# Stretches of a two-layer graph kernel ordered by a clock per engine, the first pair's addend rows made by TensorE, the other rows' transfers on the sync queue

## The chip, the cores and the metric

The kernel runs on one core of one Trainium2 chip. The metric is the device time of one execution in microseconds. All runs used here were in the fast state; most executions of one kernel agree within 0.3%. A profile's span is some 2 us shorter than the time of the run that it was taken from.

## The reference, cut to what matters

64 graphs of 256 nodes with 256 features go through two layers. Layer one is two graph attentions (GAT), a layer norm and a feed-forward with Relu; layer two is an attention with 8 heads, a layer norm and a feed-forward with Gelu.

```python
# layer 0, twice: graph attention
e = leaky_relu(Wh1 + swapaxes(Wh2, 1, 2), 0.2)
att = softmax(where(adj > 0, e, NEG), axis=1);  h = att @ Wh
# ... layer norm, Relu feed-forward of width 1024, layer norm
# layer 1: attention of 8 heads, masked by adj == r, for r in 0..3
# ... layer norm, Gelu feed-forward of width 1024, layer norm
```

## The kernel before

The kernel takes the graphs in 32 pairs. Each pair is a Python generator that emits its instructions in stretches; `in_turn` keeps three pairs under way and picks, at every `yield`, whose stretch comes next. This fixes the order of instructions on each engine when the program is built. A `yield us, later, needs` says how long TensorE is thought to take and how long after that the pair can go on.

```python
    def in_turn(ways, together):
        now, going = 0.0, []
        # ... fill `going` with up to `together` pairs
            ready = [g for g in able if g[1] <= now] or [min(able, key=lambda g: g[1])]
            g = min(ready, key=lambda g: g[2] == "ff" or alone.get("ff") is g[0])
            # ...
            us, later, needs = step
            now = max(now, g[1]) + us
            g[1:] = now + later, needs
```

A GAT's weights need one exponential per node along a row, the same on all 128 partitions. They are formed as a column, turned on VectorE, written to DRAM and read back replicated:

```python
    def addends(y, at, layer, pair):
        # ...
        for b in range(2):
            e1 = y[:, of_graph(b), at]
            nc.scalar.activation(of_kind[:, 2 * b], e1, AF.Exp, bias=shift[:, 0:1])
            nc.scalar.activation(of_kind[:, 2 * b + 1], e1, AF.Exp, bias=shift[:, 0:1], scale=ALPHA)
        nc.scalar.activation(ratio, y[:, :, at + 1], AF.Exp, scale=ALPHA - 1.0)
        blocks = small.tile([P, 2, 32], F32, name="blocks")
        nc.vector.transpose(blocks.rearrange("p j c -> p (j c)"), rise.rearrange("p j c -> p (j c)"))
        row = scratch.tile([2, 16, 32], F32, name="row")
        nc.gpsimd.dma_start(row.rearrange("j q c -> q j c"), blocks[0:P:8])
        rows = work.tile([P, 8, 4, 32], F32, name="rows")
        nc.gpsimd.dma_start(rows.rearrange("p q n c -> p (q n c)"), row.rearrange("j q c -> (j q c)").partition_broadcast(P))
        return rows, ratio
```

Feed-forwards and attention begin with rows transposed on TensorE and copied out of PSUM by ScalarE. That copy, `yT`, matters below, and so does the activation of the feed-forward, whose function is Relu in layer one and Gelu in layer two:

```python
    def rows_transposed(y, needs):
        yT = work.tile([P, KC, 512], F32, name="yT", bufs=3)
        for b in range(2):
            # ... four nc.tensor.transpose into pt
            nc.scalar.activation(yT[:, :, b * N:(b + 1) * N], pt.rearrange("p (c n) -> p c n", c=KC), AF.Copy)
            yield 0.5, 0.5 + b * 0.8, needs if b else None
        return yT

    def feed_forward(y, w, func, gb):
        # ...
            nc.scalar.activation(h, p1, func, bias=b1[:, m:m + 1])
```

## Time and profile before

| | before |
|---|---|
| time, median of the first 3 runs (lowest to highest) | 3348.53 us (3345.63 to 3352.18) |
| span of the profile | 3344.5 us |
| TensorE busy | 3283.8 us, 98% |
| longest waits of TensorE | 18.3 and 14.2 us, both in the first pair |
| one pair in the middle | some 101.9 us |

How to read it: TensorE is full but for 60.7 us, and the two waits are more than half of that. The prediction shows the lines that carry this. One group that it did not look at is ScalarE's loading of function tables. In this view of groups (line, engine, operation, count, then busy us and mean ns, then idle time before) the kernel before has:

```profile
L343 ACT ACT_TABLE_LOAD x75 | 96.2, 1283 | 6.6 <-PE ps L340 5.3
L397 ACT ACT_TABLE_LOAD x46 | 59.0, 1283 | 0.8
L223 ACT ACT_TABLE_LOAD x28 | 35.9, 1283 | 0.5
```

A switch from Exp to Gelu or back costs ScalarE 1.28 us each time, 150 times in all with the load at the start. No wait of TensorE in the middle follows from them here.

### The profile page before, as it was taken

The page shows a single profiled execution, that of the slowest core. Times are in us where ns is not written, and L with a number is a line of the kernel's source. Part 1 is how long each engine was busy: PE and PEld are TensorE (multiplying, and loading weights), DVE is VectorE, ACT ScalarE, POOL GpSimd, SP SyncE. Part 2 cuts the span into 40 slices and gives each one's busy share as a digit, 9 for nine tenths or more (in the row PEclk, how much of TensorE's full clock was granted, in tenths as well). Part 3 has the DMA queues.
Part 4 walks back from the last instruction along what each step waited for, and adds up shares of the span by engine and source line. Part 5 has one row for each costly group of instructions (what it writes and reads, how often), then busy time and mean ns, then how long its engine had stood idle before and what let it go on. Part 6 is the DMA issues. An engine that isn't in the chain of part 4 may idle for free.

```text
span 3344.5 us, 45688 instructions
## 1 busy us (share of the span) xinstructions
PE 3283.8 (98%) x18270; PEld 2106.0 (63%) x18270; DVE 1836.8 (55%) x4835; ACT 1263.6 (38%) x2326; POOL 275.7 (8%) x390
## 2 busy tenths in 40 slices
PE   4999999999999999999999999999999999999998
PEld 3666666666665656666666666566666666666665
DVE  3655465654555654556545656545555455665444
ACT  2334333343433343333343333443344433434422
POOL 0000010000000000100000100001000001000000
PEclk7999999999999999999999999999999999999999
DMA  6000111010111011110011110101110010100000
GB/s 190 32 7 32 39 38 32 20 32 32 39 35 36 13 36 35 39 32 25 28 32 38 39 32 14 38 32 38 32 32 20 32 39 32 39 7 26 20 7 14
DMA packets 78556, 111.95 MB, mean 33 GB/s; under 512 B 6784, under 2 KB 61184, under 8 KB 78336
## 3 DMA queue, kind: packets, MB, share of 16 engines
q1 hardware_dynamic: 67072, 75.13, 7.2%
q0 software_dynamic: 11264, 33.82, 2.9%
q8 instruction: 146, 2.39, 0.3%
q14 instruction: 74, 0.61, 0.1%
HBM read 91.90 MB, written 17.04 MB: 33 GB/s over the span
## 4 chain that ended last, share of the span: by engine, by line
PE 94%; DMA 3%; DVE 2%; ACT 1%; issue 0%; POOL 0%; SPq 0%; POOLq 0%; DVEq 0%
PE ps L351 26%; PE ps L340 25%; PE ps L420 6%; PE ps L367 6%; PE ps L374 6%; PE ps L392 4%; PE ps L413 4%; PE ps L289 4%; PE ps L261 3%; PE ps L437 3%; PE ps L274 3%; PE ps L327 2%; DMA rows<-row 1%; DMA adjT<-in_adjT 1%; DMA row<-blocks 1%; DVE e L240 0%
## 5 line engine op out<-in xcount | busy, mean ns | idle before, releaser
L340 PE MATMUL ps<-yT,w_L_gnn_W 128*128 128x512 f32 x1024 | 471.6, 597 | 0.7 <-ACT yT L329 0.7
L351 PE MATMUL ps<-w_L_gnn_W,ff 128*128 128x256 f32 x2048 | 457.9, 379 | 0.0
L351 PE MATMUL ps<-w_L_gnn_w_ff,ff 128*128 128x256 f32 x2048 | 455.2, 379 | 0.0
L340 PE MATMUL ps<-yT,w_L_gnn_w_ff 128*128 128x512 f32 x1024 | 452.7, 595 | 0.7 <-ACT yT L329 0.7
L351 PEld LDWEIGHTS ps<-w_L_gnn_w_ff,ff 128*128 128x128 f32 x2048 | 389.0, 190 | 66.6 <-issue 15.3
L351 PEld LDWEIGHTS ps<-w_L_gnn_W,ff 128*128 128x128 f32 x2048 | 384.3, 190 | 51.8 <-issue 2.1
L312 POOL TENSOR_TENSOR rstd<-rstd,mhalf 128x2 f32<-128x2 f32 x256 | 202.9, 793 | 2493.2 <-DVE rstd L311 2478.5
L397 ACT ACTIVATE a<-ps 128x512 f32<-128x512 f32 x512 | 264.3, 602 | 350.1 <-PE ps L392 349.9
L406 DVE TENSOR_TENSOR m<-a,adjT 128x512 f32<-128x512 f32 x512 | 325.2, 685 | 120.3 <-ACT a L397 107.3
L302 DVE TENSOR_TENSOR x<-ps,x 128x512 f32<-128x512 f32 x256 | 172.2, 673 | 330.7 <-PE ps L351 309.3
L340 PEld LDWEIGHTS ps<-yT,w_L_gnn_w_ff 128*128 128x128 f32 x1024 | 192.8, 191 | 218.1 <-issue 208.2
L329 ACT ACTIVATE yT<-ps 128x512 f32<-128x512 f32 x192 | 113.8, 594 | 566.1 <-PE ps L327 564.6
L340 PEld LDWEIGHTS ps<-yT,w_L_gnn_W 128*128 128x128 f32 x1024 | 183.7, 190 | 185.7 <-issue 176.7
L343 ACT ACTIVATE ff<-ps,c_L_gnn_b 128x512 f32<-128x512 f32 x256 | 175.6, 686 | 327.3 <-PE ps L340 326.8
L240 DVE SCALAR_TENSOR_TENSOR e<-rows,ratio 128x256 f32<-128x256 f32 x256 | 116.3, 477 | 322.7 <-DMA rows<-row 314.8
L343 ACT ACTIVATE ff<-ps,c_L_gnn_b_ff 128x512 f32<-128x512 f32 x256 | 175.9, 687 | 269.6 <-PE ps L340 269.5
L369 DVE TENSOR_TENSOR v<-ps,b_L_gnn_bv 128x512 f32<-128x512 f32 x128 | 87.5, 684 | 286.4 <-PE ps L367 286.4
L367 PE MATMUL ps<-wv,yT 128*128 128x512 f32 x512 | 235.4, 592 | 0.0
L426 DVE RECIPROCAL s<-ps 128x256 f32<-128x256 f32 x128 | 224.1, 1751 | 0.0
L309 DVE BATCH_NORM_STATS2 st<-x 128x6 f32<-128x256 f32 x512 | 192.3, 416 | 6.1
L247 ACT ACTIVATE xw<-xw,rs 128x258 f32<-128x258 f32 (+1 forms) x256 | 117.4, 502 | 144.0 <-DVE rs L244 144.0
L367 PEld LDWEIGHTS ps<-wv,yT 128*128 128x128 f32 x512 | 97.2, 190 | 114.3 <-issue 113.4
(97 smaller groups left out, 3763.9 us busy)
## 6 DMA issues: line engine op xcount, KB each, us to landing
rows<-row POOLq DMA_DIRECT2D x64, 512.0 KB, 3.9
xT<-in_xT SPq DMA_DIRECT2D x32, 512.0 KB, 4.2
adjT<-in_adjT SPq DMA_DIRECT2D x32, 512.0 KB, 3.9
x<-in_x SPq DMA_DIRECT2D x32, 512.0 KB, 3.9
out<-x SPq DMA_DIRECT2D x32, 512.0 KB, 2.9
w_L_gnn_w_ff<-in_L_gnn_w_ff SPq DMA_DIRECT2D x2, 1024.0 KB, 9.6
w_L_gnn_W<-in_L_gnn_W SPq DMA_DIRECT2D x2, 1024.0 KB, 11.6
row<-blocks POOLq DMA_DIRECT2D x64, 4.0 KB, 1.9
```

The lines of the kernel that those rows point to most:

```text
L302: nc.vector.tensor_tensor(rows, p, rows, ALU.add)
L309: nc.vector.bn_stats(st[:, j, :], r[:, 2 * b + j, :])
L312: nc.gpsimd.tensor_tensor(rstd, rstd, mhalf[:, :2], ALU.pow)
L340: nc.tensor.matmul(p1, lhsT=w1[:, c, m * P:(m + 1) * P], rhs=yT[:, c, :], start=c == 0, stop=c == KC - 1)
L343: nc.scalar.activation(h, p1, func, bias=b1[:, m:m + 1])
L351: nc.tensor.matmul(p2[:, j * D:(j + 1) * D], lhsT=f[m][:, k * P:(k + 1) * P], rhs=w2[:, m, :], start=m == 0, stop=m == NF - 1)
L367: nc.tensor.matmul(ps, lhsT=yT[:, c, at:at + P], rhs=wv[:, c].rearrange("p r m -> p (r m)"), start=c == 0, stop=c == KC - 1)
L374: nc.tensor.matmul(ps, lhsT=w[:, d, c * P:(c + 1) * P], rhs=yT[:, d, :], start=d == 0, stop=d == KC - 1)
L397: nc.scalar.activation(a, ps[o], AF.Exp)
L406: nc.vector.tensor_tensor(m, a, adj, ALU.mult)
L420: nc.tensor.matmul(po[o * DH:(o + 1) * DH, :N], lhsT=v[:, jc, at:at + DH], rhs=ms[o][:, jc * N:(jc + 1) * N], start=r == 0 and jc == 0, st ...
L426: nc.vector.reciprocal(s, po[:, N:])
```

## The change

It has three parts. Part 1: the rows of the first pair, which has no other work to stand beside its transfers, come from TensorE: a transpose of a broadcast column yields the same row on all partitions. Part 2: the order follows a clock per engine. A stretch reports when each engine would be done with its results, and the pair goes on then. Part 3: the other pairs' row transfers are issued on the sync queue in place of GpSimd's. The diff, cut to its core:

```diff
+    clock = {"tensor": 0.0, "vector": 0.0, "scalar": 0.0, "gpsimd": 0.0}
+    def took(us):
+        clock["tensor"] += us
+        return clock["tensor"]
+    def after(ready, *work):
+        for engine, us in work:
+            ready = clock[engine] = max(ready + 0.2, clock[engine]) + us
+        return ready
 # in in_turn
-            ready = [g for g in able if g[1] <= now] or [min(able, key=lambda g: g[1])]
+            ready = [g for g in able if g[1] <= clock["tensor"]] or [min(able, key=lambda g: g[1])]
 # in addends
+        if pair == 0:
+            for n in range(4):
+                p = bank()
+                for j in range(2):
+                    nc.tensor.transpose(p[:, j * P:(j + 1) * P], rise[:, j, 8 * n:8 * n + 1].to_broadcast([P, P]), ident)
+                nc.scalar.activation(rows[:, :, n], p[:, :N].rearrange("p (q c) -> p q c", q=8), AF.Copy)
+            return rows, ratio, after(took(1.6), ("scalar", 2.0))
-        nc.gpsimd.dma_start(row.rearrange("j q c -> q j c"), blocks[0:P:8])
-        nc.gpsimd.dma_start(rows.rearrange("p q n c -> p (q n c)"), row.rearrange("j q c -> (j q c)").partition_broadcast(P))
-        return rows, ratio
+        nc.sync.dma_start(row.rearrange("j q c -> q j c"), blocks[0:P:8])
+        nc.sync.dma_start(rows.rearrange("p q n c -> p (q n c)"), row.rearrange("j q c -> (j q c)").partition_broadcast(P))
+        return rows, ratio, after(clock["tensor"], ("scalar", 2.2), ("vector", 0.4)) + 6.6
 # in feed_forward; the other yields change alike
-            yield 1.72, 0.0, None
+            there = after(took(1.72), ("scalar", 0.7))
+            yield clock["tensor"] if m < NF - 1 else max(clock["tensor"], there - 3.0), None
 # ... cut: the same for gat_layers, layernorm, rows_transposed, attention, whole_way
```

The clock counts 0.7 us of ScalarE for a feed-forward tile. It knows no function tables.

More of the change, by code (lines that the diff above doesn't have):

```diff
@@ L174, in relieve_attention, with each_after @@
         nc.vector.tensor_tensor(bv, bv, p, ALU.subtract)
+    clock = {"tensor": 0.0, "vector": 0.0, "scalar": 0.0, "gpsimd": 0.0}
     alone = {}
+    def took(us):
[5 more added lines that the diff above has]
+        return ready
+    def each_after(ready, times, *work):
+        for _ in range(times):
+            end = after(ready, *work)
+        return end
     def in_turn(ways, together):
-        now, going = 0.0, []
-        ways = iter(ways)
+        going, ways = [], iter(ways)
         while True:
@@ L196, in in_turn @@
                 alone[g[2]] = g[0]
+            clock["tensor"] = max(clock["tensor"], g[1])
             step = next(g[0], None)
@@ L199, in in_turn @@
                 going.remove(g)
-                continue
-            us, later, needs = step
-            now = max(now, g[1]) + us
-            g[1:] = now + later, needs
+            else:
+                g[1:] = step
     def done_with(name):
@@ L225, in addends @@
         nc.scalar.activation(ratio, y[:, :, at + 1], AF.Exp, scale=ALPHA - 1.0)
+        rows = work.tile([P, 8, 4, 32], F32, name="rows")
+        if pair == 0:
[5 more added lines that the diff above has]
+            return rows, ratio, after(took(1.6), ("scalar", 2.0))
         blocks = small.tile([P, 2, 32], F32, name="blocks")
@@ L228, in addends @@
         row = scratch.tile([2, 16, 32], F32, name="row")
-        nc.gpsimd.dma_start(row.rearrange("j q c -> q j c"), blocks[0:P:8])
-        rows = work.tile([P, 8, 4, 32], F32, name="rows")
-        nc.gpsimd.dma_start(rows.rearrange("p q n c -> p (q n c)"), row.rearrange("j q c -> (j q c)").partition_broadcast(P))
-        return rows, ratio
+        nc.sync.dma_start(row.rearrange("j q c -> q j c"), blocks[0:P:8])
+        nc.sync.dma_start(rows.rearrange("p q n c -> p (q n c)"), row.rearrange("j q c -> (j q c)").partition_broadcast(P))
+        return rows, ratio, after(clock["tensor"], ("scalar", 2.2), ("vector", 0.4)) + 6.6
     def gat_weights(y, at, rows, ratio, adjT, empty, b):
@@ L247, in gat_weights @@
             nc.scalar.activation(y[:, k, :at], y[:, k, :at], AF.Copy, scale=rs[:, j:j + 1])
-        return e
+        return e, after(clock["tensor"], ("vector", 2.3), ("scalar", 1.0))
     def gat_layers(pair, xT, adjT, x):
@@ L263, in gat_layers @@
                 nc.scalar.activation(y[:, k], ps[:, :D + 4], AF.Copy)
+            took(1.75)
             if b == 0:
-                yield 1.75, 0.0, None
-        rows, ratio = addends(y, D + 2, 0, pair)
-        yield 1.75, 8.6, None
+                yield clock["tensor"], None
+        rows, ratio, there = addends(y, D + 2, 0, pair)
+        yield there, None
         e = [gat_weights(y, D + 2, rows, ratio, adjT, empty, b) for b in range(2)]
-        yield 0.0, 4.6, None
+        yield e[0][1], None
         for b in range(2):
@@ L273, in gat_layers @@
                 for j in range(2):
-                    nc.tensor.matmul(ps[:, :D + 2], lhsT=e[b][:, j, i * P:(i + 1) * P], rhs=y[:, 2 * b + j, :D + 2],
+                    nc.tensor.matmul(ps[:, :D + 2], lhsT=e[b][0][:, j, i * P:(i + 1) * P], rhs=y[:, 2 * b + j, :D + 2],
                                      start=j == 0, stop=j == 1)
                 nc.scalar.activation(z[:, 2 * b + i, :D + 2], ps[:, :D + 2], AF.Copy)
+            took(1.75)
             if b == 0:
-                yield 1.75, 0.4, None
-        rows, ratio = addends(z, D, 1, pair)
+                yield e[1][1], None
+        rows, ratio, there = addends(z, D, 1, pair)
         if pair + 1 < NPAIR:
             loaded[pair + 1] = load(pair + 1)
-        yield 1.75, 8.6, None
-        e += [gat_weights(z, D, rows, ratio, adjT, empty, b) for b in range(2)]
-        yield 0.0, 4.6, None
+        yield there, None
+        e = [gat_weights(z, D, rows, ratio, adjT, empty, b) for b in range(2)]
+        yield e[0][1], None
+        normal = []
         for b in range(2):
@@ L288, in gat_layers @@
                 for j in range(2):
-                    nc.tensor.matmul(ps[:, i * D:(i + 1) * D], lhsT=e[2 + b][:, j, i * P:(i + 1) * P],
+                    nc.tensor.matmul(ps[:, i * D:(i + 1) * D], lhsT=e[b][0][:, j, i * P:(i + 1) * P],
                                      rhs=z[:, 2 * b + j, :D], start=j == 0, stop=j == 1)
+            took(1.75)
             add_rows(x, ps, b)
-            layernorm(x, ln[0], b)
+            normal.append(layernorm(x, ln[0], b))
             if b == 0:
-                yield 1.75, 0.4, None
+                yield e[1][1], None
         done_with("gat")
-        yield 1.75, 6.0, None
+        return normal
     def add_rows(y, p, b):
@@ L318, in layernorm, with rows_transposed @@
             nc.vector.scalar_tensor_tensor(row, row, rstd[:, j:j + 1], beta, op0=ALU.mult, op1=ALU.add)
-    def rows_transposed(y, needs):
+        return after(clock["tensor"], ("vector", 2.0), ("gpsimd", 1.0), ("vector", 1.8))
+    def rows_transposed(y, normal, needs):
         yT = work.tile([P, KC, 512], F32, name="yT", bufs=3)
         for b in range(2):
+            yield normal[b], None
             pt = bank()
@@ L329, in rows_transposed, with feed_forward @@
             nc.scalar.activation(yT[:, :, b * N:(b + 1) * N], pt.rearrange("p (c n) -> p c n", c=KC), AF.Copy)
-            yield 0.5, 0.5 + b * 0.8, needs if b else None
+            there = after(took(0.45), ("scalar", 0.6))
+        yield there, needs
         return yT
-    def feed_forward(y, w, func, gb):
+    def feed_forward(y, normal, w, func, gb):
         w1, b1, w2 = w
-        yT = yield from rows_transposed(y, "ff")
+        yT = yield from rows_transposed(y, normal, "ff")
         f = []
@@ L352, in feed_forward @@
                                      start=m == 0, stop=m == NF - 1)
-                if k < 3:
-                    if j == 1:
-                        add_rows(y, p2, b)
-                        layernorm(y, gb, b)
-                    yield 3.44, 0.0, None
-        add_rows(y, p2, 1)
-        layernorm(y, gb, 1)
+                took(3.44)
+                if j == 0:
+                    yield clock["tensor"], None
+            add_rows(y, p2, b)
+            normal[b] = layernorm(y, gb, b)
+            if b == 0:
+                yield clock["tensor"], None
         done_with("ff")
@@ L369, in values @@
         nc.vector.tensor_tensor(v[:, jc], ps, bv, ALU.add)
+        return after(took(1.72), ("vector", 0.7))
     def projected(to, c, yT, w, bias, scale):
@@ L375, in projected, with attention @@
         nc.scalar.activation(to[:, c, :], ps, AF.Identity, bias=bias[:, c:c + 1], scale=scale)
-    def attention(y, pair, adjT):
-        yT = yield from rows_transposed(y, "attention")
+        return after(took(1.72), ("scalar", 0.7))
+    def attention(y, normal, pair, adjT):
+        yT = yield from rows_transposed(y, normal, "attention")
         qT, kT, oT = (work.tile([P, KC, 512], F32, name=n) for n in ("qT", "kT", "oT"))
@@ L398, in scores @@
                 e.append(a)
+            took(0.95)
             return e
@@ L407, in of_relation_1 @@
                 ms.append(m)
-            return ms
+            return ms, each_after(clock["tensor"], HQ, ("scalar", 0.62), ("vector", 0.62))
         def sums(e, po):
@@ L430, in divided @@
             nc.vector.tensor_tensor(oT[:, c, b * N:(b + 1) * N], po[:, :N], s, ALU.mult)
+            return after(clock["tensor"], ("vector", 2.6))
         def into_rows(b):
@@ L438, in into_rows @@
                                      start=c == 0, stop=c == KC - 1)
+            took(1.72)
             add_rows(y, ps, b)
-        groups = [(b, c) for b in range(2) for c in range(KC)]
+        divisions, groups = [], [(b, c) for b in range(2) for c in range(KC)]
         v = values_tile()
         projected(qT, 0, yT, wq, bqs, SCALE)
-        projected(kT, 0, yT, wk, bk, 1.0)
-        yield 3.44, 0.0, None
+        there = projected(kT, 0, yT, wk, bk, 1.0)
+        yield clock["tensor"], None
         values(v, 0, 0, yT)
-        yield 1.72, 0.0, None
+        yield there, None
         e = scores(*groups[0])
-        ms = of_relation_1(0, e)
+        ms, masked = of_relation_1(0, e)
         projected(qT, 1, yT, wq, bqs, SCALE)
-        yield 3.0, 0.0, None
-        projected(kT, 1, yT, wk, bk, 1.0)
-        values(v, 1, P, yT)
-        yield 3.44, 0.0, None
+        yield clock["tensor"], None
+        there = projected(kT, 1, yT, wk, bk, 1.0)
+        there = max(there, values(v, 1, P, yT), masked)
+        yield there, None
         for n, (b, c) in enumerate(groups):
@@ L463, in attention @@
             if not last:
-                e, ms = ahead, of_relation_1(groups[n + 1][0], ahead)
-            divided(b, c, po)
-            if last:
-                layernorm(y, ln[2], 0)
-            yield 3.1 if last else 4.1, 4.8 if last else 0.8, None
+                e, (ms, masked) = ahead, of_relation_1(groups[n + 1][0], ahead)
+            took(2.65)
+            divisions.append(divided(b, c, po))
             if n == 0:
@@ L471, in attention @@
                 for jc in range(2):
-                    values(following, jc, N + jc * P, yT)
-                    yield 1.72, 0.0, None
+                    yield clock["tensor"], None
+                    there = values(following, jc, N + jc * P, yT)
             if n == 1:
@@ L476, in attention @@
             if n == 2:
+                yield divisions[1], None
                 into_rows(0)
-                yield 1.75, 0.0, None
+            if last:
+                normal[0] = layernorm(y, ln[2], 0)
+            yield divisions[3] if last else max(masked, there), None
         into_rows(1)
-        layernorm(y, ln[2], 1)
+        normal[1] = layernorm(y, ln[2], 1)
         done_with("attention")
-        yield 1.75, 6.0, None
     def whole_way(pair):
-        yield 0.0, 0.0, "gat"
+        yield 0.0, "gat"
         xT, adjT, x = loaded.pop(pair)
-        yield from gat_layers(pair, xT, adjT, x)
+        normal = yield from gat_layers(pair, xT, adjT, x)
         if pair == 0:
             relieve(ff0[1], ff0[0], ln[0][2])
-        yield from feed_forward(x, ff0, AF.Relu, ln[1])
-        yield 3.44, 6.0, None
+        yield from feed_forward(x, normal, ff0, AF.Relu, ln[1])
         if pair == 0:
             relieve_attention(ln[1][2])
-        yield from attention(x, pair, adjT)
+        yield from attention(x, normal, pair, adjT)
         if pair == 0:
             relieve(ff1[1], ff1[0], ln[2][2])
-        yield from feed_forward(x, ff1, AF.Gelu, ln[3])
-        yield 3.44, 5.0, None
+        yield from feed_forward(x, normal, ff1, AF.Gelu, ln[3])
+        yield max(normal), None
         nc.sync.dma_start(out[2 * pair:2 * pair + 2].rearrange("b (c p) d -> p (b c) d", p=P), x)
```

## The prediction

> **What bounds the kernel now.** I read four views in order: the page's busy table and slices, who waited for whom on TensorE, TensorE's timeline in the first 100 us, and the chain of waits at the end.
>
> ```profile
> PE 3283.8 (98%) x18270; PEld 2106.0 (63%) x18270; DVE 1836.8 (55%) x4835; ACT 1263.6 (38%) x2326; POOL 275.7 (8%) x390
> ...
> PE   4999999999999999999999999999999999999998
> ...
> PEclk7999999999999999999999999999999999999999
> ```
>
> TensorE (PE) is busy for 3283.8 of 3344.5 us, so all that a better order can win without removing matmuls is the rest, 60.7 us, or 1.8% of the time. The second row says where most of it lies: 38 of 40 slices are full, the first (83.6 us) is 4 tenths busy. In two inner periods of 101.8 us that I measured (1710 to 1913.6 us), PE was busy for 203.43 of 203.60 us.
>
> ```profile
> PE ps L274 <- ACT xw L247: 18.3, 1, 18.3
> PE ps L289 <- ACT xw L247: 14.2, 1, 14.2
> PE pw L121 <- DVE junk L115: 7.5, 1, 7.5
> PE ps L327 <- DVE x L318: 1.9, 1, 1.9
> PE ps L340 <- ACT yT L329: 1.4, 2, 0.7
> ```
>
> Columns: waiter, releaser, total us, times, longest. Two single waits make 32.5 us. They name ScalarE's scaling (L247), but that is only the last link; the timeline of PE dates them:
>
> ```profile
> 12.17 5.41 PE L261 MATMUL ps<-w,xT 128*128 128x260 f32 x16 [0.84 <-DVE w L123]
> 35.83 5.50 PE L274 MATMUL ps<-xw,e 128*128 128x258 f32 x16 [18.26 <-ACT xw L247]
> 55.52 5.86 PE L289 MATMUL ps<-xw,e 128*128 128x256 f32 x16 [14.20 <-ACT xw L247]
> 61.22 3.67 PE L261 MATMUL ps<-w,xT 128*128 128x260 f32 x16
> ...
> 72.59 11.00 PE L340 MATMUL ps<-yT,w_L_gnn_w_ff 128*128 128x512 f32 x20 [0.69 <-ACT yT L329]
> ```
>
> and the chain of waits, in order of time, gives the real cause:
>
> ```profile
> 24.06 8.90 DMA rows<-row
> ...
> 33.07 0.88 DVE e L240 x2
> 33.95 0.81 DVE e L242 x4
> 34.76 0.40 DVE e L240
> 35.16 0.09 DVE rs L244
> ...
> 35.27 0.52 ACT xw L247
> ...
> 42.83 5.19 DMA row<-blocks
> ...
> 48.57 4.09 DMA rows<-row
> ```
>
> The addend rows of the first pair go out to DRAM and back, 512 KB replicated over 128 partitions, while the weights load (the stretch 20 to 40 us moves 282 GB/s). Only the first pair has no other work to put beside that. From 72.59 us on PE never waits long until its last matmul ends at 3330.0 us; the 14.5 us after that are the last layer norm, the store and the closing check.
>
> **What the Trainium skill says.** "DMA: Bandwidth & Descriptors", Issuing engines are not separate DMA queues: transfers issued by sync, scalar or gpsimd run on the same 16 engines, and another issuer saves only issue time. I therefore expect nothing from the queue move in itself; the trace has 3.9 us for 512 KB rows from GpSimd and 3.9 to 4.2 us for 512 KB loads from sync. "TensorE: Matmul & The Clock Gate", Part 4: PE-mode transpose: the result lands in PSUM and must be copied out. The trace agrees: L327 is followed by an ACT copy; four transposes take 0.44 us of the chain. Same page, The HAM clock gate: an idle window of some 3.4 us halves the clock. The trace agrees: the granted clock was 0.50 in the first 1.8 us of L274 and L289, and 0.57 before; eight matmuls took 5.5 and 5.86 us there against 3.5 us when warm.
>
> **The change, part by part.** (1) *First pair's rows on TensorE.* It removes, twice, a block transpose on DVE and two DMAs, and adds 8 transposes (0.11 us each, some 1.8 us for 16) and 4 ACT copies of 128x256 from PSUM (0.39 us, the duration of the 128x260 copy). I lay the new head out from measured durations and the instruction order of the built kernel.
>
> Layer 1: L261's matmuls end at 17.6 as now. ACT copies the last tile to 18.0, the first row to 18.4, forms the last exponentials (0.48) and the ratio (0.15), then three rows at some 0.38 each, to 20.2. DVE needs only the first two rows to begin, at 19.5. Its 2.2 us (33.07 to 35.25 now) and 0.55 of scaling put the first weighted sum at 22.3 instead of 35.83. Half cold it takes some 4.7: 27.0.
>
> Layer 2: copy 0.45, row copy 0.4, exponentials and ratio 0.65, second row 0.35: DVE starts at 28.9. In its order two weight subtractions and a bias one (L137, L140; 0.4 each) now stand in between, and parts of the second graph, so the reciprocal is ready at 32.65; scaling: PE starts at 33.2 instead of 55.52. Cold again, 5.2 us: 38.4 instead of 61.38. Then the bias relief (3.48) and the next pair's projection (3.5): 45.4. The second layer norm waits behind the relief on DVE (42.1) and needs 3.3: also 45.4. Transposes 0.55 and 0.45, copy 0.6: the first feed forward starts at 47.0 instead of 72.59. Same work done by then, so **25.5 us saved**.
>
> (2) *Order by a clock per engine.* No matmul beyond the 16 transposes is added; only the order changes. The number of switches between full, row-tiled, column-tiled and transposing stretches goes from 773 to 757 for all pairs; the dear ones (a full matmul after column-tiled ones takes 1.92 instead of 1.72 us for a pair) go up by 19, those into transposes go down by 19. I count it as zero. Within the inner periods I checked the new distances: from a projection to its weighted sum PE has 16.4 us of other work where the rows take 9 to 11.5 us and weights and scaling 2.7; a layer norm (4.1 us) before its transposes has 5.6. One place is tight: DVE does 3.6 us of GAT weights ahead of a layer norm, ready by my count 15.0 us after a sum whose transposes come at 15.9. With nothing to win in the middle (2 us of idle), this part can mainly cost: +1.5 us.
>
> (3) *Rows on the sync queue.* For the second pair sync issues one 512 KB input ahead of the row and two ahead of the rows: blocks ready at 48.3, rows landed at about 56, weights 2.8 later, 59; PE gets there at 47.0 + 14 x 0.86 = 59.1. Allowance +1.5. Later, a store's completion (2.9) and an input load stand before a pair's rows; inside the 16.4 us above.
>
> (4) *Tail.* The last transposes now stand between feed-forward matmuls, so the 0.69 us wait before the last L340 goes: -0.7. At the start of attention a copy of 0.6 is no longer covered: +0.7.
>
> Sum: -25.5 + 1.5 + 1.5 - 0.7 + 0.7 = -22.5 us, so 3348.5 - 22.5 = **3326 us**.
>
> **Rivals.** *A: the head saves less.* Something else could end the wait: the next pair's input, issued at 32.70 and landing some 6 us later, or the weights. Against: projection two is due only at 41.9, and without the 512 KB in the queue the loads come sooner. If the input came 6 us later than needed, 3332. *B: sync's in-order queue becomes the wait.* A row behind a store and two loads would stall PE in each pair. For: every row now stands behind one. Against: 16.4 us of cover. If each pair lost 1 us, 3348 and nothing is gained; 2 us, 3380, slower. *C: steady gain.* If the old order hid slow spots inside "busy", the new one could win more, say 0.3 us a pair: 3316. Against: a period is 101.8 us with the same matmuls in both.
>
> **Range and chances.** The head is the firmest term (20 to 28). Stalls of 0 to 0.5 us a pair in the middle give 0 to 16 us on the other side. So 3315 to 3342. Faster by over 2% needs under 3281.6 us, which is more than all idle time of PE: 1 in 100. Slower by over 2% needs 2.8 us lost in every pair: 1 in 100. Within 2%: 98.
>
> **What would show it.** Right: PE's first weighted sum near 22 us, the second near 33, L340's successor near 47; PE busy about 3285 us, the span shorter by the lost idle. A wait of PE on rows around 59 us would size term (3). Wrong: PE idle of more than 5 us in total between 110 and 3300 us, with layer norms or rows as releasers (B, or the tight place), a head later than 52 us (A), or a period other than 101.8 us (C).

## The result, and the profile after

Six runs of the changed kernel had a median of 3346.06 us (3343.69 to 3350.78), six of the kernel before in the same comparison 3347.9 us. The ratio is 0.9995, with a 95% interval of 0.9982 to 1.0008. Here and below a ratio is the mean time of one kernel's fast runs over that of the other's fast runs of the same rounds, so it is not quite the ratio of the medians. The change does not move the time.

The page after, busy time and slices:

```profile
PE 3284.7 (98%) x18286; PEld 2113.6 (63%) x18286; DVE 1844.7 (55%) x4833; ACT 1434.0 (43%) x2464; POOL 202.6 (6%) x262
...
PE   7999999999999999999999999999999999999998
...
PEclk9999999999999999999999999999999999999999
```

The first slice went from 4 to 7 tenths, as meant, and TensorE's busy time is what it was plus 0.9 us. ScalarE's (ACT) grew from 1263.6 to 1434.0 us. The timeline of TensorE shows the head:

```profile
11.66 3.77 PE L285 MATMUL ps<-w,xT 128*128 128x260 f32 x16 [0.52 <-DVE w L123]
15.31 0.62 PE L248 MATMUL ps<-ident,rise 128*128 128x128 f32 x4
...
19.67 5.44 PE L299 MATMUL ps<-xw,e 128*128 128x258 f32 x16 [2.65 <-ACT xw L271]
...
30.75 5.41 PE L316 MATMUL ps<-xw,e 128*128 128x256 f32 x16 [4.05 <-ACT xw L271]
35.99 4.81 PE L162 MATMUL ps<-c_L_gnn_b_ff2c,w_L_gnn_w_ff 128*128 128x1 f32 x32
40.67 5.89 PE L285 MATMUL ps<-w,xT 128*128 128x260 f32 x16
...
48.62 12.28 PE L371 MATMUL ps<-yT,w_L_gnn_w_ff 128*128 128x512 f32 x28 [1.19 <-ACT yT L359]
```

The first feed-forward begins at 48.62 us in place of 72.59. (Line numbers moved: the weighted sums L274 and L289 are L299 and L316 now, the feed-forward's L340 is L371, the attention's projections L374 are L407, the copy L329 is L359. L374 is now the feed-forward's activation.) So 24 us were won there, and the waits of TensorE say where they went (waiter, releaser: total us, times, longest):

```profile
PE ps L407 <- ACT yT L359: 29.3, 16, 1.9
PE pw L121 <- DVE junk L115: 7.4, 1, 7.4
PE ps L316 <- ACT xw L271: 4.1, 1, 4.1
PE ps L299 <- ACT xw L271: 2.6, 1, 2.6
PE ps L426 <- ACT kT L408: 1.5, 1, 1.5
```

The two long waits of the first pair are down to 2.6 and 4.1 us. In their place stands a wait that the kernel before had only in small: 16 times the attention's first projection waits for ScalarE's copy of its transposed rows, once 1.1 us in the first pair and then 15 times 1.88 us, in every second pair. (The expectations below speak of 16 waits of 1.88 us.) TensorE's timeline at one such place:

```profile
881.66 1.90 PE L299 MATMUL ps<-xw,e 128*128 128x258 f32 x8
883.40 1.88 PE L371 MATMUL ps<-yT,w_L_gnn_W 128*128 128x512 f32 x4
885.12 1.90 PE L299 MATMUL ps<-xw,e 128*128 128x258 f32 x8
...
889.01 1.88 PE L371 MATMUL ps<-yT,w_L_gnn_W 128*128 128x512 f32 x4
892.78 1.98 PE L407 MATMUL ps<-yT,w_L_gnn_Wq 128*128 128x512 f32 x4 [1.88 <-ACT yT L359]
894.60 1.88 PE L407 MATMUL ps<-yT,w_L_gnn_Wk 128*128 128x512 f32 x4
```

and ScalarE's in the same microseconds:

```profile
882.05 0.69 ACT L374 ACTIVATE ff<-ps,c_L_gnn_b 128x512 f32<-128x512 f32 x1
...
884.01 1.28 ACT L240 ACT_TABLE_LOAD   x1
885.30 0.30 ACT L240 ACTIVATE rise<-xw,shift 128x2 f32<-128x2 f32 x1
885.62 1.28 ACT L374 ACT_TABLE_LOAD   x1
886.91 0.69 ACT L374 ACTIVATE ff<-ps,c_L_gnn_b 128x512 f32<-128x512 f32 x1
...
888.17 1.28 ACT L241 ACT_TABLE_LOAD   x1
...
890.25 1.28 ACT L374 ACT_TABLE_LOAD   x1
891.55 0.69 ACT L374 ACTIVATE ff<-ps,c_L_gnn_b 128x512 f32<-128x512 f32 x1
892.13 0.59 ACT L359 ACTIVATE yT<-ps 128x512 f32<-128x512 f32 x1
```

The new order puts the second GAT's exponentials (`rise`) among the Gelu tiles of another pair (`ff`), and one Gelu even between the exponentials. ScalarE changes tables four times from 884 us on, 5.1 us of loading, works without a break, and reaches the copy 3.1 us after the transposes that it copies were done (889.02 in the chain of waits). The old order had the same exponentials beside matmuls of the Relu feed-forward, which need no load; only afterwards came one load for Gelu, with 2.87 us of idle time behind it:

```profile
1712.31 0.30 ACT L223 ACTIVATE rise<-xw,shift 128x2 f32<-128x2 f32 x1
1712.52 0.28 ACT L224 ACTIVATE rise<-xw,shift 128x2 f32<-128x2 f32 x1
1712.91 1.28 ACT L343 ACT_TABLE_LOAD   x1
1717.06 0.69 ACT L343 ACTIVATE ff<-ps,c_L_gnn_b 128x512 f32<-128x512 f32 x1 [2.87 <-PE ps L340]
```

The groups count it over the whole kernel, after:

```profile
L374 ACT ACT_TABLE_LOAD x140 | 179.6, 1283 | 16.7 <-PE ps L371 14.3
L431 ACT ACT_TABLE_LOAD x109 | 139.8, 1283 | 2.0
L240 ACT ACT_TABLE_LOAD x15 | 19.2, 1283 | 0.3
L241 ACT ACT_TABLE_LOAD x15 | 19.2, 1283 | 0.3
```

There are 280 loads with the one at the start, 130 more than before; 130 x 1.28 = 167 us, which is nearly all of ScalarE's growth of 170 us.

Two more things came to light. First, three of the 15 waits of 1.88 us are followed by a stretch at half the granted clock. These are windows of 2 us (window, length, TensorE's busy time and instructions, clock, share of the DMA engines, GB/s):

```profile
1302.00:1304.00 2.00, 0.71 (x2) 1.00 0.11 37
1304.00:1306.00 2.00, 2.00 (x4) 0.63 0.60 227
1306.00:1308.00 2.00, 2.00 (x3) 0.51 0.00 0
1308.00:1310.00 2.00, 2.00 (x6) 1.00 0.00 0
```

Such a drop costs 1.7 us (the two pairs around it took 206.95 us where others took 205.25) and shows in no list of waits, as TensorE counts as busy. I summed 1 minus the clock over all windows of 5 us from 110 us on: 5.2 us lost after, 0 before.

Second, the last store is issued at 3333.97 us of 3344.5 before,

```profile
3333.97 0.37 SPq L499 DMA_DIRECT2D out<-x  x1
```

and at 3337.06 of 3342.1 after,

```profile
3337.06 0.37 SPq L535 DMA_DIRECT2D out<-x  x1
```

that is 10.5 and 5.0 us ahead of the end. With three cuts (the head up to the first feed-forward matmul, by when the same work is done in all kernels; the middle up to the issue of the last store; the end) the spans add up:

| us in the profile | head | middle | end | span |
|---|---|---|---|---|
| before | 72.6 | 3261.4 | 10.5 | 3344.5 |
| after | 48.6 | 3288.4 | 5.0 | 3342.1 |
| difference | -24.0 | +27.1 | -5.5 | -2.4 |

A wait costs more than its idle time. The stretches of four matmuls above start 1.72 us apart but last 1.88; from 889.01 to 894.60 are 5.59 us in place of 3.44, so this wait cost 2.15. Two pairs take 205.25 us with a wait and 203.11 without (e3 and e5 below), 2.14 each. So the middle's +27.1 is 33.2 of waits (15 x 2.14 and the first pair's 1.1) and 5.2 of halved clock, less some 11.3 us that something in the new order must have saved.

### The profile page after: what moved, and what is told of

Same layout as the page of the kernel before. It is cut to its first block, busy times and chain, and to the rows that moved or that the text cites. A ratio compares the mean times of both kernels' runs of the same rounds, so it can differ in the third digit from the quotient of the medians.

```text
span 3342.1 us, 45806 instructions
## 1 busy us (share of the span) xinstructions
PE 3284.7 (98%) x18286; PEld 2113.6 (63%) x18286; DVE 1844.7 (55%) x4833; ACT 1434.0 (43%) x2464; POOL 202.6 (6%) x262
## 4 chain that ended last, share of the span: by engine, by line
PE 94%; ACT 4%; DVE 1%; DMA 0%; issue 0%; POOL 0%; SPq 0%; POOLq 0%; DVEq 0%
PE ps L383 27%; PE ps L371 24%; PE ps L407 7%; PE ps L399 7%; PE ps L455 7%; PE ps L426 4%; PE ps L448 4%; PE ps L473 3%; PE ps L285 3%; PE ps L316 3%; PE ps L299 3%; PE ps L357 2%; ACT L374 1%; ACT ff L374 1%; ACT L241 1%; ACT L240 1%
## 5 line engine op out<-in xcount | busy, mean ns | idle before, releaser
L371 PE MATMUL ps<-yT,w_L_gnn_W 128*128 128x512 f32 x1024 | 473.3, 595 | 0.0
L371 PE MATMUL ps<-yT,w_L_gnn_w_ff 128*128 128x512 f32 x1024 | 457.4, 594 | 1.2 <-ACT yT L359 1.2
L340 POOL TENSOR_TENSOR rstd<-rstd,mhalf 128x2 f32<-128x2 f32 x256 | 201.9, 789 | 3132.9 <-DVE rstd L339 3119.2
L374 ACT ACTIVATE ff<-ps,c_L_gnn_b_ff 128x512 f32<-128x512 f32 x256 | 175.6, 686 | 417.1 <-PE ps L371 416.8
L359 ACT ACTIVATE yT<-ps 128x512 f32<-128x512 f32 x192 | 111.9, 591 | 514.4 <-PE ps L357 514.4
L371 PEld LDWEIGHTS ps<-yT,w_L_gnn_w_ff 128*128 128x128 f32 x1024 | 189.6, 190 | 208.4 <-issue 201.7
L374 ACT ACTIVATE ff<-ps,c_L_gnn_b 128x512 f32<-128x512 f32 x256 | 174.4, 687 | 322.4 <-PE ps L371 321.4
L371 PEld LDWEIGHTS ps<-yT,w_L_gnn_W 128*128 128x128 f32 x1024 | 187.1, 190 | 187.2 <-issue 173.0
L234 DVE TENSOR_REDUCE steep<-xw 128x1 f32<-128x8 f32 x64 | 10.3, 161 | 357.9 <-ACT xw L301 204.7
L374 ACT ACT_TABLE_LOAD x140 | 179.6, 1283 | 16.7 <-PE ps L371 14.3
## 6 DMA issues: line engine op xcount, KB each, us to landing
w_L_gnn_W<-in_L_gnn_W SPq DMA_DIRECT2D x2, 1024.0 KB, 10.5
```

The costliest lines, as they stand in the source:

```text
L340: nc.gpsimd.tensor_tensor(rstd, rstd, mhalf[:, :2], ALU.pow)
L371: nc.tensor.matmul(p1, lhsT=w1[:, c, m * P:(m + 1) * P], rhs=yT[:, c, :], start=c == 0, stop=c == KC - 1)
```

## The experiments

Theory T: the new order brings ScalarE's table loads ahead of the attention's copy, and those waits eat what the head won. Rivals: R1, the head's gain is not real because the second pair is then late; R2, the sync queue makes the waits; R3, it is the place of the stretches or VectorE, not the table loads. I compared the order of TensorE's instructions in each experiment with that of its parent: all are equal, but for the first pair's transposes where those are added or taken out. A median is of the experiment's own runs; "before" is the kernel before in the same rounds. Ten of the twelve kernels passed as correct; the other two (e3, e4) give a wrong result on purpose.

### e1: part 1 alone

```diff
 # the kernel before, in addends
+        if pair == 0:
+            # ... the transposes and copies of the change
+            return rows, ratio
```

> Part 1 alone: the kernel before with only the first pair's rows made by TensorE; TensorE's order is that of before plus 16 transposes. Theory T (the new order eats the head's gain through activation table loads on ScalarE that delay the copy before the attention's first projections): without the new order nothing is eaten, so 20 to 25 us faster than before, 3323 to 3328 us, and no waits of 1.88 us on that copy. Rival R1 (the head's gain is not real, because in what follows the second pair's rows are then late): within 5 us of before, with a new long wait on the second pair's weighted sum.

Measured: 3323.77 us against 3347.33, ratio 0.993 (0.9913 to 0.9946). Its profile has a head of 49.1, a middle of 3262.3 and an end of 10.4 us. In the old order the head's gain stays: 23.5 us less head, 23.6 us less time. R1 falls; the only new wait of over 1 us is one of 2.3 us on the second pair's input.

### e2: part 2 alone

```diff
 # the changed kernel, in addends
-        if pair == 0:
-            # ... the transposes and copies
-        nc.sync.dma_start(...)   # both row transfers
+        nc.gpsimd.dma_start(...)
```

> Part 2 alone: the changed kernel without the transposes for the first pair and with the DMAs of the rows on GpSimd again. T: the head as slow as before and 16 waits of 1.88 us added, so 25 to 30 us slower than before, 3373 to 3378 us, ratio about 1.008. Rival R2 (the sync queue makes the waits): as before, 3345 to 3350 us, no waits of 1.88 us.

Measured: 3380.89 us, ratio 1.0101 (1.0084 to 1.0117), slower even than expected. The waits are there without the sync queue, so R2 does not explain them:

```profile
PE ps L400 <- ACT yT L352: 29.4, 16, 2.0
PE ps L309 <- ACT xw L264: 16.3, 1, 16.3
PE ps L292 <- ACT xw L264: 16.3, 1, 16.3
```

(The first line is the same copy and projection under this kernel's numbers.) The halved clock took 10.2 us here, which I had not put into the expectation.

### e3 and e4: no table loads, in the new order and in the old

```diff
-        yield from feed_forward(x, normal, ff1, AF.Gelu, ln[3])
+        yield from feed_forward(x, normal, ff1, AF.Relu, ln[3])
```

e3 is the changed kernel with this line, e4 the kernel before with the like. Both give a wrong result on purpose. ScalarE's program has 3 loads in each in place of 282 and 152 (two of these belong to a fallback path that is not run).

> Wrong result on purpose: the changed kernel with Relu in place of Gelu in the second feed forward, so that ScalarE has 3 table loads in its program in place of 282; TensorE's order is the same, instruction for instruction. T: the 16 waits of 1.88 us vanish, 27 to 31 us faster than the changed kernel, 3315 to 3319 us. Rival R3 (the waits come from the place of the stretches or from VectorE, not from the table loads): the waits stay, 3343 to 3348 us.

> Control for the one above, wrong on purpose too: the kernel before with Relu in place of Gelu. T: its 152 table loads are hidden, TensorE waited only some 2 us in the middle, so 0 to 3 us faster than before, 3345 to 3348 us. If it is 10 us or more faster, table loads cost time in the old order as well and T's accounting is wrong.

Measured: e3 3309.15 us, ratio 0.9883 (0.9866 to 0.9899); e4 3347.05 us, ratio 1.0001 (0.9992 to 1.001). So the loads cost nothing in the old order, and 37 us (3346.06 - 3309.15) in the new, more than the 29 of idle time in the waits. In e3's waits the line on the copy is down to the one of the first attention:

```profile
PE ps L426 <- ACT kT L408: 1.4, 1, 1.4
PE ps L371 <- ACT yT L359: 1.2, 1, 1.2
PE ps L407 <- ACT yT L359: 1.1, 1, 1.1
```

R3 falls: the place of the stretches is the same and VectorE's work too. The surplus is the true cost of a wait and the halved clock that went with the waits (5.2 to 1.7 us): 15 x 2.14 + 3.5 = 35.6 us, and the two profiles' spans differ by 35.5 (3342.1 - 3306.6).

### e5: the copy on VectorE

```diff
 # the changed kernel, in rows_transposed
+            if needs == "attention":
+                nc.vector.tensor_copy(yT[:, :, b * N:(b + 1) * N], pt.rearrange("p (c n) -> p c n", c=KC))
+            else:
                 nc.scalar.activation(yT[:, :, b * N:(b + 1) * N], ...)
```

> The changed kernel with the copy of the attention's transposed rows from PSUM on VectorE in place of ScalarE; the 282 table loads stay, TensorE's order is the same. T: the copy no longer queues behind the loads, so the wait before the first projection goes, but the copies of queries and keys still come from ScalarE, which is some 2 us behind: 15 to 29 us faster than the changed kernel, 3317 to 3331 us, with at most a small wait left on the keys' copy. Rival R3 (it is not ScalarE's queue): no change, 3343 to 3348 us.

Measured: 3308.85 us (3308.36 to 3311.2), ratio 0.9887 (0.987 to 0.9903), correct, and better than expected. All 280 loads are still there, but what TensorE needs first no longer queues behind them. Its waits:

```profile
PE ps L410 <- DVE yT L360: 3.2, 1, 3.2
PE ps L299 <- ACT xw L271: 2.6, 1, 2.6
...
PE ps L429 <- ACT kT L411: 0.3, 1, 0.3
```

TensorE waits for the keys' copy, which I had feared, once, for 0.3 us, and at none of the 15 places. This is the fastest of the correct versions.

### e6: the four exponentials as one instruction

```diff
+        expo = small.tile([P, 4, 2], F32, name="expo")
         for b in range(2):
             e1 = y[:, of_graph(b), at]
-            nc.scalar.activation(of_kind[:, 2 * b], e1, AF.Exp, bias=shift[:, 0:1])
-            nc.scalar.activation(of_kind[:, 2 * b + 1], e1, AF.Exp, bias=shift[:, 0:1], scale=ALPHA)
+            nc.vector.tensor_copy(expo[:, 2 * b], e1)
+            nc.vector.tensor_scalar(expo[:, 2 * b + 1], e1, ALPHA, None, ALU.mult)
+        nc.scalar.activation(of_kind, expo, AF.Exp, bias=shift[:, 0:1])
```

> The changed kernel with the four exponentials of the rows as one ScalarE instruction (VectorE lays out and scales its input), so that a Gelu can no longer fall between them: 252 table loads in place of 282, two fewer in each of the 15 spots that wait; TensorE's order the same. T: 2.56 us less on ScalarE ahead of a copy that comes 1.88 us late, so all the waits go: 26 to 30 us faster than the changed kernel, 3316 to 3320 us. Rival R3: no change, 3343 to 3348 us.

Measured: 3323.72 us, ratio 0.9928 (0.9911 to 0.9944), correct. This missed the expectation by some 4 us: the waits shrank and did not go (here 15 of 0.81 us and a shorter one in the first pair).

```profile
PE ps L409 <- ACT yT L361: 12.9, 16, 0.8
```

Two loads fewer are 2.56 us, but the wait fell from 1.88 to 0.81, by 1.07. The timeline says why: in the changed kernel the first exponential's load ran from 884.01, in time that ScalarE had free; with one instruction it has to wait for the last tile of its input and starts at 885.43. I had counted ScalarE's work and not when it can begin. Half the dose still gave a good part of the effect, and none of the 0.81 us waits was followed by a halved clock (1.7 us lost in all, at one place, see the last section).

### e7, e8 and e9: the queue

e7 is the changed kernel with `nc.gpsimd` for the row transfers again, e8 is e1 with `nc.sync` for them, and e9 is the kernel before with `nc.sync` alone.

```diff
-        nc.gpsimd.dma_start(row.rearrange("j q c -> q j c"), blocks[0:P:8])
-        nc.gpsimd.dma_start(rows.rearrange("p q n c -> p (q n c)"), ...)
+        nc.sync.dma_start(row.rearrange("j q c -> q j c"), blocks[0:P:8])
+        nc.sync.dma_start(rows.rearrange("p q n c -> p (q n c)"), ...)
```

> Part 3 undone: the changed kernel with the rows' DMAs on GpSimd again; TensorE's order the same. T: rows are not what TensorE waits for, so the same as the changed kernel, 3343 to 3349 us, 16 waits of 1.88 us. Rival R2 (the sync queue costs): 5 us or more faster.

> Parts 1 and 3 without part 2: the kernel before with the first pair's rows by TensorE and the others' DMAs on the sync queue, old order. T: as the head alone, 3321 to 3328 us, no waits on the copy. Rival R2: slower than the head alone by 5 us or more, with waits on rows.

> Part 3 alone: the kernel before with the rows' DMAs on the sync queue, old order, nothing else. Seen so far: kernels with the rows on GpSimd end 10.4 to 10.6 us after their last store is issued, those on sync 5.0 to 5.2 us. Theory Q (the queue's gain is all at the end of the program): 5 us faster than before, 3341 to 3344 us, with the middle and the head unchanged. Rival (the gain lies in the middle, rows landing earlier): the end as before, and less waiting of TensorE in the middle, which is only 2 us in all, so 0 to 2 us.

Measured: e7 3358.62 us, ratio 1.0033 (1.0022 to 1.0044), so 12.6 us slower than the changed kernel where I had expected no difference (11.2 against e12, which ran on the same chip), and in the direction opposite to R2. e8 3316.11 us, ratio 0.9909 (0.9893 to 0.9926), 7.7 us faster than e1, which ran on another chip (there the kernel before took 3347.33 us, here 3347.81). e9 3344.82 us, ratio 0.9987 (0.998 to 0.9994), some 4 us faster than before.

| us in the profile | head | middle | end |
|---|---|---|---|
| before (GpSimd) | 72.6 | 3261.4 | 10.5 |
| e9 (sync) | 77.6 | 3259.4 | 5.0 |
| e1 (GpSimd) | 49.1 | 3262.3 | 10.4 |
| e8 (sync) | 46.6 | 3262.0 | 5.2 |
| after (sync) | 48.6 | 3288.4 | 5.0 |
| e7 (GpSimd) | 48.5 | 3299.1 | 10.4 |

The end is 5.2 to 5.5 us shorter in every one of the three comparisons; e8's other 2.5 us are in its head, where e1's wait of 2.3 us on the input is gone. That confirms the first half of e9's theory; its second half, a head unchanged, was wrong. In the old head the first pair's row now stands behind the weights in sync's program. Before, GpSimd issued it here:

```profile
19.10 0.67 POOL L229 DMA_DIRECT2D row<-blocks  x1 [17.77 <-DMA c_L_gnn_boc<-in_L_gnn_boc]
```

and in e9 sync issues it here, 13 us later:

```profile
32.07 0.58 SPq L229 DMA_DIRECT2D row<-blocks  x1
```

So part 3 gives its full gain only with part 1: without rows of the first pair to transfer, nothing is late. Of e7's middle, 10.6 us longer, 6.7 are more halved clock (11.9 against 5.2); the other 4 I did not trace to a cause.

### e10 and e11: the order without its waits, and a control for the copy

e10 is e2 with e5's copy on VectorE. e11 is e8 with that copy.

```diff
 # e10 on e2, e11 on e8: in rows_transposed, as in e5
+            if needs == "attention":
+                nc.vector.tensor_copy(...)
+            else:
                 nc.scalar.activation(...)
```

> Part 2 alone with the copy of the attention's rows moved to VectorE; rows by DMA from GpSimd for all pairs. Theory S (without its waits the new order is itself a little faster in the middle: two pairs took 203.1 us in the run with the copy on VectorE, some 203.8 us before): 15 double pairs by 0.7 us, 10 us faster than before, 3336 to 3340 us. Rival: the new order gains nothing in itself, and the copy's run owed its time to head and queue alone: 3346 to 3350 us.

> Control for the copy on VectorE: parts 1 and 3 in the old order, with the copy of the attention's rows on VectorE too. T: there was no wait on this copy in the old order, so the same as without it, 3314 to 3318 us. Rival (the copy on VectorE is a gain of its own): 5 us faster or more.

Measured: e10 3343.03 us, ratio 0.9981 (0.9974 to 0.9987); e11 3323.05 us, ratio 0.992 (0.9904 to 0.9935). e10 is faster than before, by 6 us and not by 10. Two pairs take 203.1 us in the middle of its profile as in e5, against 203.3 to 204.6 before; but its first store comes 4.0 us later than e2's, with a head 1.5 us longer, a longer halved clock at 170 us (3.4 against 1.7 us) and the 3.2 us wait of the first copy. e11 refutes the idea that the copy on VectorE is a gain of its own: in the old order it costs 7 us against e8 by the medians, and some 4 by the ratios to the kernel before. Of its middle, 8 us longer in the profile of the slowest of its four runs, 3.8 are waits for the copy and 2.6 one wait on an input; the rest is open.

### e12: the changed kernel again

```diff
 # no edit
```

> The changed kernel once more, on the chip of the others. T: 16 waits of 1.88 us again, at the same places; the halved clock after a wait, seen after 3 of the 16 in the first profile, is a matter of chance, so 1 to 7 times here, at other places. 3342 to 3351 us. Rival (the drops are fixed by the program): the same three places.

Measured: 3347.47 us, ratio 0.9996 (0.9988 to 1.0005). Again 16 waits, 29.4 us. The clock halved after four of them, at 483, 1305, 1923 and 2746 us, where the first profile had it at 1304, 2127 and 2950; one place is common to both. So the waits belong to the program, and where the drops fall differs between executions, which fits the changed kernel's spread of 7 us over runs (3343.69 to 3350.78) against 2.8 us of e5 (3308.36 to 3311.2).

Within an execution the drops are not chance. In each of these traces the records of the granted clock, of which the view of windows shows averages, change on one grid of 3.4133 us, to within 0.01 us. The four profiles with this wait (the changed kernel twice, e2 and e7) hold 60 gaps of 1.87 to 1.98 us. Eighteen of them began 0.10 to 1.06 us after a point of the grid, and after each of these the clock was halved from the next point on; the other 42 began elsewhere on the grid, and after none of them was it. As two pairs take 205.25 us, which is 60 steps of the grid (204.80) and 0.45 us more, the wait moves along the grid and meets the bad part every few times.

## Why the prediction was right or wrong

**Part 1, the head: right.** 25.5 us were predicted, 24.0 measured in the changed kernel, 23.5 in e1's head and in its time. Inside, two errors cancelled in part. The first weighted sum came at 19.67 us (22.3 predicted) and the second at 30.75 (33.2), because the first projection took 3.77 us where the kernel before had 5.41. Then the bias relief and the next projection ran at a lower clock, 4.81 and 5.89 us in place of the 3.48 and 3.5 that I took from the warm trace (the clock was halved from 38.2 to 45.0 us). One reading of the prediction is loose: the 0.57 "before" the sums is the mean of 20 to 40 us, which contains the first of them; the record of the clock has 0.50 from 22.3 to 39.4 us.

**Part 2, the order: wrong, and this is the step that failed.** The prediction said that "this part can mainly cost: +1.5 us", on distances checked for row transfers, layer norms and VectorE. ScalarE's queue and its table loads are in none of these. Yet the copy that came late stands in part 4 ("a copy of 0.6 is no longer covered: +0.7"): it was counted once and as a bare copy, not as the last in a queue. The runs showed 29.3 us of waits behind the table loads, which cost 33.2, and 5.2 us of halved clock behind the waits. Rival B was right that the middle can take everything back; its cause, sync's queue, was not it, and its sum was off: 1 us in each of 32 pairs on top of 3326 us is 3358, not 3348. Some 0.7 us a pair would have used up the 22.5; waits and clock took 1.2. The test named for B, over 5 us of idle in the middle, is what showed the loss, only with the copy as releaser and neither rows nor layer norms. It could have been seen blind: the instruction order of the built kernel lists every table load, 282 against 152, and a load's 1283 ns stands in the profile of before.

**The order's own gain: predicted as zero, some 11 to 13 us.** e5's middle is 3253.7 us and e3's 3253.0 against 3261.4, though these two hold 1.7 us of halved clock and the first pair's wait for the copy (3.2 and 1.1 us), which the kernel before has not; net of these they gain 12.6 and 11.2. Two pairs took 203.11 us in both, and 203.88 before on average. This is rival C at 0.4 us a pair, near the 0.3 that it named. The distances between starts over ten pairs show where: in e5 the weighted sums took 69.3 us (72.4 before) and the output projections 36.0 (38.1). Which neighbours make them slower in the old order is not settled.

**Part 3, the queue: wrong.** "I expect nothing from the queue move in itself", with an allowance of +1.5. In place of it stood -5.5 us at the end of the program, a place that I had put down to "the last layer norm, the store and the closing check" and not examined. The tight place at 59 us was computed well: the second pair's sums started at 60.74, straight after the matmuls before them, without a wait.

**Part 4: the tail as said, the copy not.** The last wait of L340 is gone. The first attention's projection waits 1.13 us (0.7 allowed), but the same copy is 1.88 us late at 15 later places, as said under part 2.

**The sum.** -24.0 + 33.2 + 5.2 - 11.3 - 5.5 = -2.4 us of span, in place of -22.5; the 11.3 is what is left of the middle (27.1 us longer) once the waits and the clock are counted. e3's middle, 8.4 us shorter with 2.8 us of wait and halved clock in it, confirms its size. That the result came within 20 us of the prediction is in part luck: two gains that it did not foresee (11.3 and 5.5) hid part of a loss that it did not foresee either (38.4). With the waits taken away (e5) the same change gives 3308.85 us, better than the 3326 predicted, as the two terms that I put at zero both gain.

## What to carry to other kernels

An engine that is 40% busy can still hold up the bound one, if the order makes it switch function tables ahead of what is needed next: count table loads in the built order, not only busy time, whenever two activation sets meet. A model that orders work needs the switch as a cost; short of that, the copy on the critical path goes to an engine that does not switch (in the old order, where nothing was late, the same move cost time: e11). And test the parts of a change alone: here one gained 24 us, one 4 and one lost 33, and the sum looked like nothing at all.

## What the Trainium skill lacked or had wrong

- "ScalarE: Activation LUTs", What ACT_TABLE_LOAD costs: some 1283 ns for the load and some 1380 ns of drain, 2.66 us for a switch; the section Table sets works its example with this sum, about 2.7 us. The runs agree on the load (1283 ns for 280 loads) and show no drain: in the lines above the load of 888.17 starts when the work before it ends (888.16), and the next activation starts at 889.47, 1.30 us later. The page's rule to batch activations by set is what this change broke: the change cost 29.3 us of waits at 16 places. The page does not say that the stall reaches another engine through a plain copy queued behind the loads.
- "TensorE: Matmul & The Clock Gate", Part 1: an idle window of about 3.4 us, which is free-running, brings the clock down. The runs show that a gap of 1.88 us can be enough: half clock after 3 of 15 such gaps in one profile and after 4 of 15 in another, each time at a cost of about 1.7 us, and always when the gap began 0.10 to 1.06 us after a point of the clock's grid (18 of 60 gaps in four profiles). After 15 gaps of 0.81 us there was none.
- The same page has no word on how matmuls of one column count for the clock gate: in e1 32 of them (3.63 us, from 143.55 us) were followed by a half clock at 148.2 us, with TensorE busy throughout. Eleven of the 14 profiles have such a drop 3.0 to 4.9 us after the start of these matmuls; the kernel before, e4 and the changed kernel's first profile have none. That such matmuls count as little activity is inferred from this, and no run tests it.
- "DMA: Bandwidth & Descriptors", Issuing engines are not separate DMA queues: another issuer is said to save only issue time. The runs show 5.2 to 5.5 us less from the last store's issue to the end of the program when GpSimd issues no transfers at all (4.9 to 5.2 against 10.4 to 10.5 us). Which step of the ending takes it, the trace does not show.
